# Last feed-forward of a four-layer decoder: its weight work placed beside the cross-attention's units, its output bias added to x by GpSimd

## The chip, the cores and the metric

One core of one Trainium2 chip runs the whole decoder as one program. The metric is the device time of one execution in microseconds; lower is better. Before the change three executions took 3528.01, 3537.2 and 3549.08 us, so the median is 3537.2 us.

## The reference, cut to what matters

The decoder has four layers, each with self-attention, cross-attention and feed-forward, all of the form `x = x + f(layernorm(x))`, on x of 16 x 128 tokens with 256 features in 32-bit floats. The change concerns the end of layer 3. The cross-attention ends with `out @ Wo + bo`. The feed-forward is two linear layers with a GELU between. Each linear layer rounds its weights to 8 bits with one scale for the whole matrix, and adds a low-rank product:

```
def fake_quant_weight(w, bits=8):
    qmax = 2.0 ** (bits - 1) - 1
    scale = jnp.max(jnp.abs(w)) / qmax
    wq = jnp.clip(jnp.round(w / scale), -qmax - 1, qmax) * scale
    return w + stop_gradient(wq - w)

def qat_lora_linear(x, W, b, A, B):        # SCALING = 2
    base = einsum('bsi,oi->bso', x, fake_quant_weight(W)) + b
    lora = einsum('bsr,or->bso', einsum('bsi,ri->bsr', x, A), B)
    return base + SCALING * lora

h = gelu(qat_lora_linear(hidden_states, W_fc, b_fc, A_fc, B_fc))      # 256 -> 1024
h = qat_lora_linear(h, W_proj, b_proj, A_proj, B_proj)                # 1024 -> 256
```

The rank is 16. The kernel folds the low-rank part into the weights: it computes A^T B^T once per weight block and adds twice of it to the rounded block.

## The kernel before, in words

**Tiling.** The 16 sequences are four groups (`NG = 4`) of four (`GB = 4`), 128 tokens each. `self.x[g]` holds the rows of group g, 128 partitions by 4 x 256 features, in SBUF for the whole program. Products are in 32-bit floats; each such matmul of the program appears in the trace as two PE instructions. Small PSUM tiles (`b1`, 128 x 512) rotate through four buffers, so a fifth one waits until the first has been read.

**Order of the instructions.** Each engine works through its own queue in order. A scheduler orders the instructions of a queue from the program; those given to `keep_in_program_order` (through `pinned`, `pinned_transpose` or directly) stay in the order in which they were written. The order that came out of it can be listed per engine, and the prediction uses that of both kernels.

**The last cross-attention** (`xattn64` with 8 heads, called by `l3_xattn`). Sixteen units, one per sequence, are numbered m = 0 to 15. The loop runs m from 0 to 17: iteration m holds on PE the sums of unit m-1 (`sums`, tile d), the scores of unit m (st), the values of unit m-1 (o), the reciprocal row sums spread over the heads (rb), the maxima entered into st, the score products for the next maxima (s), and the projection of unit m-2 (proj). DVE takes the reciprocal r of d (L1200), on which rb waits; multiplies o by rb to cT (L1215), on which the next projection waits; takes the maxima nm of s (L1156), on which st waits in the next iteration; and adds proj to x (L222). ScalarE copies rb (L1213) and takes the exponentials e (L1173). At m = 2, 6 and 10 the next group's prologue follows: keys, the layer norm's transposes (tr), queries and values, with copies by DVE and ScalarE (`evac` alternates between them), bf16 casts kb and qb by GpSimd (L1127, L1135) and the bias `bo` added to x by GpSimd (L1130). `begin` is a function that starts the following feed-forward's work and returns a table "after iteration m do this"; layer 1 uses it (`l1_ffn_begin`: a reduction of each weight, L1281, and roundings, L1294, L1297), layers 2 and 3 do not.

**The last feed-forward** (`l3_ffn`). Loads of the two weights are issued early into slots that the self-attention's last tiles leave free. Everything else starts when the cross-attention's pool closes:

- four loads of the low-rank factors (L2657);
- the largest absolute value of each weight on DVE (L2661), across partitions by a GpSimd `partition_all_reduce` (L2666), scales sc and inv (L2667, L2668);
- three passes of rounding and clipping over each weight, 128 x 2048 (L2671 to L2673);
- 4 low-rank products of 512 columns and 8 of 256 (tile lora), each added to its block by DVE (L2681);
- per group g: layer norm and transposes to hT, 8 blocks of fc with two matmuls each and a GELU to y (L2689), then 4 tiles pr of eight matmuls and one more that adds the bias, from a row of ones and the bias row (L170, in `mm`), `add_x` (L222), and one transfer of x[g] to the output (L2694).

In the order that came out, the layer-norm statistics of groups 0 to 2 and the normalised rows of groups 0 and 1 already stand beside the cross-attention's units; the transposes of all four groups stand after it.

Of the kernel before, what the change touches and what calls it, by code (L numbers as in the profile page):

```python
# [9 lines left out]
F = mybir.dt.float32  # L10
# [3 lines left out]
ALU = mybir.AluOpType  # L14
AX = mybir.AxisListType
PSUM = bass.MemoryType.PSUM

P = 128
B = 16
T = B * P  # L20
DM = 256
DC = 192
NG = 4
GB = B // NG
GT = GB * P
EPS = 1e-5
MAGIC = 12582912.0
# [3 lines left out]
class Decoder:  # L31
# [2611 lines left out]
                finish(*f)  # L2643

    def l3_xattn(self):
        self.xattn64(8, [f"L3_xattn_{n}" for n in ("Wq", "Wk", "Wv", "Wo")], "L3_xattn_bo", "l3x")

    def l3_ffn(self):
        nc = self.nc
        ws = [self.load("L3_W_fcT"), self.load("L3_W_projT")]  # L2650
        bp = self.row("L3_ffn_b_proj")
        outv = self.out.rearrange("(g b s) d -> g s b d", b=GB, s=P)
        with self.tc.tile_pool(name="l3f", bufs=1) as wk:
            lora = {}
            for n, shape in (("A_fc", DM), ("BT_fc", 1024), ("A_proj", 1024), ("BT_proj", DM)):
                lora[n] = wk.tile([16, shape], F, tag=n, name=n)
                nc.sync.dma_start(out=lora[n], in_=self.a[f"L3_{n}"])  # L2657

            mx = wk.tile([P, 2], F, tag="mx", name="mx")
            for i, w in enumerate(ws):  # L2660
                nc.vector.tensor_reduce(  # L2661
                    mx[:, i : i + 1], w.rearrange("p c n -> p (c n)"), AX.X, ALU.max, apply_absolute_value=True
                )
            sc = wk.tile([P, 2], F, tag="sc", name="sc")
            inv = wk.tile([P, 2], F, tag="inv", name="inv")
            nc.gpsimd.partition_all_reduce(sc, mx, P, bass_isa.ReduceOp.max)  # L2666
            nc.vector.tensor_scalar(sc, sc, 1.0 / 127.0, None, ALU.mult)  # L2667
            nc.vector.reciprocal(inv, sc)  # L2668
            for i, (w, a, b) in enumerate(((ws[0], "A_fc", "BT_fc"), (ws[1], "A_proj", "BT_proj"))):
                flat = w.rearrange("p c n -> p (c n)")  # L2670
                nc.vector.tensor_scalar(flat, flat, inv[:, i : i + 1], MAGIC, ALU.mult, ALU.add)  # L2671
                nc.vector.tensor_scalar(flat, flat, -MAGIC, 127.0, ALU.add, ALU.min)
                nc.vector.tensor_scalar(flat, flat, -128.0, sc[:, i : i + 1], ALU.max, ALU.mult)  # L2673
                width = w.shape[2]
                step = min(width, 512)
                for c in range(w.shape[1]):
                    for o in range(0, width, step):
                        ps = self.b1("lora")[:, 0:step]
                        self.mm(ps, [(lora[a][:, c * P : (c + 1) * P], lora[b][:, o : o + step])])
                        wt = w[:, c, o : o + step]  # L2680
                        nc.vector.scalar_tensor_tensor(wt, ps, 2.0, wt, ALU.mult, ALU.add)  # L2681
            wf, wp = ws
            for g in range(NG):
                hT = self.hidden_T(self.layernorm(g))
                y = wk.tile([P, 8, GT], F, tag="y", name="y", bufs=2)
                for c in range(8):
                    ps = self.b1("fc")
                    self.mm(ps, [(wf[:, k, c * P : (c + 1) * P], hT[:, k, :]) for k in range(2)])
                    nc.scalar.activation(y[:, c, :], ps, AF.Gelu, bias=self.c("L3_b_fc")[:, c : c + 1])  # L2689
                for t in range(GB):  # L2690
                    po = self.b1("pr")[:, 0:DM]
                    self.mm(po, [(y[:, c, t * P : (t + 1) * P], wp[:, c, :]) for c in range(8)], bp)
                    self.add_x(g, t, po)
                nc.sync.dma_start(out=outv[g], in_=self.x[g])  # L2694


LAYERS = [
# [121 lines left out]
```

## Time and profile before

| what | value |
|---|---|
| median of the three runs | 3537.2 us |
| the profiled execution | 3545.85 us |
| its span in the trace | 3544.1 us (1.75 us lie around it) |
| its mean granted TensorE clock | 0.975 |
| busy: PE, weight loads, DVE, ScalarE, GpSimd | 3344.9, 1827.0, 2124.5, 1426.0, 426.2 us |
| last cross-attention on PE, to the end of the last proj | 3203 to 3388.2 us |
| between the last proj and the first fc | 3388.2 to 3410.9 us |
| feed-forward products to the end of the span | 3410.9 to 3544.1 us |

Times are microseconds from the start of the span of one profiled execution. PE is TensorE's matmuls, PEld its weight loads, DVE is VectorE, ACT ScalarE, POOL GpSimd, SP the engine that issues most transfers. In a timeline a line has start, duration, engine, line of the kernel, operation, output and inputs, shape, count, and in brackets how long the engine stood idle before it and what released it; "issue" there means that the profile shows nothing that it waited for. The chain of work is followed back from the last instruction, at each step to what released it. The granted clock is the share of TensorE's full clock.

### The profile page before, as it was taken

To read this page: it belongs to the slowest core of one execution; us is meant where nothing else is said; L and a number is where in the kernel's file an instruction comes from. 1 tells how busy PE (TensorE), PEld (TensorE's weight loads), DVE (VectorE), ACT (ScalarE), POOL (GpSimd) and SP (SyncE) were. 2 spreads that over 40 slices of the span, in tenths; PEclk is the share of its full clock that TensorE was granted. 3 is DMA by queue.
4 is the path that set the end of the run, shared out by engine and by line. 5 is a ranking of instruction groups with operands and counts; after the bars stand their busy time and mean duration, and the time that the engine had idled before them with its cause. 6 is when DMAs were issued, how large, how long until landed. Compare 5 with 4: busy or idle time off the path is not lost.

```text
span 3544.1 us, 51931 instructions
## 1 busy us (share of the span) xinstructions
PE 3344.9 (94%) x21208; PEld 1827.0 (52%) x21208; DVE 2124.5 (60%) x4206; ACT 1426.0 (40%) x1908; POOL 426.2 (12%) x571
## 2 busy tenths in 40 slices
PE   7999999999999999998999899978999999999989
PEld 4666655555566566664555566652222222225656
DVE  5546444444565545468677544435999999953430
ACT  2357211111124322238555322124677777783221
POOL 5411000000003211110000110223000000002100
PEclk9979999999999999999999999987999999999989
DMA  2000000000010100010200001655102020000000
GB/s 79 1 23 15 14 23 18 18 23 18 29 50 2 39 1 1 1 43 8 44 1 13 14 1 48 209 186 134 25 12 32 11 32 11 11 1 26 1 8 18
DMA packets 94118, 110.50 MB, mean 31 GB/s; under 512 B 13972, under 2 KB 74006, under 8 KB 93622
## 3 DMA queue, kind: packets, MB, share of 16 engines
q1 hardware_dynamic: 88744, 97.59, 10.4%
q0 software_dynamic: 5136, 9.60, 0.8%
q8 instruction: 167, 2.74, 0.3%
q14 instruction: 71, 0.58, 0.1%
HBM read 91.31 MB, written 15.83 MB: 30 GB/s over the span
## 4 chain that ended last, share of the span: by engine, by line
PE 79%; DVE 10%; ACT 5%; issue 3%; DMA 2%; POOL 1%; SPq 0%; POOLq 0%; ACTq 0%; DVEq 0%
PE acc L2351 7%; PE down L257 7%; PE gate L257 6%; PE up L257 6%; PE proj L257 6%; PE st L2351 5%; PE one L2351 5%; PE st L257 4%; PE qT L168 3%; PE o L257 2%; DVE mx L2497 2%; PE rb L257 2%; PE pr L168 2%; PE kT L1113 2%; PE fc L168 2%
## 5 line engine op out<-in xcount | busy, mean ns | idle before, releaser
L2497 DVE TENSOR_REDUCE mx<-one 128x1 f32<-128x512 f32 x1024 | 658.1, 686 | 55.4 <-PE one L2351 46.0
L2634 ACT ACTIVATE e<-st 128x1024 f32<-128x1024 f32 x512 | 497.1, 1021 | 204.2 <-PE st L2351 203.2
L803 ACT ACTIVATE gs<-gate,cols 128x512 f32<-128x512 f32 x132 | 90.7, 687 | 551.1 <-PE gate L257 544.1
L2351 PE MATMUL acc<-e,v 128*32 128x512 f32 x2048 | 283.7, 608 | 0.9 <-ACT e L2634 0.9
L817 DVE SCALAR_TENSOR_TENSOR x<-down,w_all,x 128x256 f32<-128x256 f32 x512 | 212.3, 477 | 110.4 <-PE down L257 110.2
L2351 PE MATMUL st<-qp,kp 113*128 113x512 bf16 x1024 | 270.6, 384 | 3.6 <-ACT e L2634 1.8
L257 PE MATMUL down<-expert,gs 128*128 128x256 f32 x1056 | 249.4, 379 | 2.2 <-DVE gs L804 2.2
L257 PE MATMUL gate<-hT,expert 128*128 128x512 f32 x528 | 248.5, 593 | 0.2 <-ACT hT L712 0.2
L257 PE MATMUL up<-hT,expert 128*128 128x512 f32 x528 | 248.1, 592 | 0.0
L257 PEld LDWEIGHTS down<-expert,gs 128*128 128x128 f32 x1056 | 200.6, 190 | 85.7 <-issue 61.5
L804 DVE SCALAR_TENSOR_TENSOR gs<-up,cols,gs 128x512 f32<-128x512 f32 x132 | 98.9, 749 | 228.7 <-PE up L257 227.9
L2351 PEld LDWEIGHTS <-qp 16*128 16x128 bf16 x1024 | 48.8, 91 | 329.2 <-issue 317.2
L2351 PE MATMUL one<-kp,qp 16*128 16x512 bf16 x1024 | 210.3, 394 | 6.9 <-DMA kp<-parts 4.2
L257 PEld LDWEIGHTS up<-hT,expert 128*128 128x128 f32 x528 | 100.3, 190 | 126.3 <-issue 126.3
L2351 PEld LDWEIGHTS <-kp 113*128 113x128 bf16 x1024 | 78.7, 98 | 140.3 <-issue 80.1
L1213 ACT COPY rb<-rb 128x512 f32<-128x512 f32 x64 | 37.5, 586 | 264.7 <-PE rb L257 264.7
L257 PEld LDWEIGHTS gate<-hT,expert 128*128 128x128 f32 x528 | 99.6, 190 | 70.3 <-issue 63.5
L1215 DVE TENSOR_TENSOR cT<-o,rb 128x512 f32<-128x512 f32 x64 | 44.2, 691 | 152.5 <-ACT rb L1213 152.5
L168 PE MATMUL qT<-hT,L_xattn_Wq 128*128 128x512 f32 x256 | 114.1, 599 | 4.8 <-DVE hT L112 4.8
L257 PE MATMUL o<-e,v 128*32 128x128 f32 (+1 forms) x2048 | 106.6, 281 | 12.6 <-DVE nm L294 11.8
L1526 DVE SCALAR_TENSOR_TENSOR xs<-xBC,cols,xs 128x508 f32<-128x508 f32 x144 | 105.9, 741 | 14.9 <-ACT xs L1522 11.6
L257 PE MATMUL proj<-L_xattn_Wo,cT 128*128 128x256 f32 x384 | 95.2, 391 | 2.8 <-DVE cT L1215 2.8
(565 smaller groups left out, 5489.4 us busy)
## 6 DMA issues: line engine op xcount, KB each, us to landing
W<-in_L_ffn_W_dram SPq DMA_DIRECT2D x58, 512.0 KB, 4.2
expert<-in_L_ffn_Wg_dram SPq DMA_DIRECT2D x32, 128.0 KB, 2.2
expert<-in_L_ffn_Wu_dram SPq DMA_DIRECT2D x32, 128.0 KB, 2.7
expert<-in_L_ffn_Wd_dram SPq DMA_DIRECT2D x32, 128.0 KB, 2.4
parts<-parts SPq DMA_DIRECT2D x16, 256.0 KB, 2.8
qp<-parts SPq DMA_DIRECT2D x28, 128.0 KB, 3.6
kp<-parts SPq DMA_DIRECT2D x12, 256.0 KB, 7.9
hs<-zero SPq DMA_DIRECT2D x21, 128.0 KB, 4.1
```

Source lines behind the costliest of these rows:

```text
L168: self.nc.tensor.matmul(out, lhsT, rhs, start=i == 0, stop=i == n - 1 and bias is None)
L257: self.tc.keep_in_program_order(self.nc.tensor.matmul(*a, **k))
L803: nc.scalar.activation(gs, pg, AF.Silu, bias=bg)
L804: nc.vector.scalar_tensor_tensor(gs, pu, bu, gs, ALU.add, ALU.mult)
L817: nc.vector.scalar_tensor_tensor(xt, pd[:, t, :], w_all[:, o : o + 1], xt, ALU.mult, ALU.add)
L1113: nc.tensor.matmul(ps, l, r, start=True, stop=False)
L1213: nc.scalar.copy(rb, ps)
L1215: nc.vector.tensor_tensor(cT, po, rb, ALU.mult)
L1526: stt = lambda *a: pin(nc.vector.scalar_tensor_tensor(*a))
L2351: self.tc.keep_in_program_order(nc.tensor.matmul(*a, **k))
L2497: nc.vector.tensor_reduce(mx[:, t, kc, i : i + 1], pair[i], AX.X, ALU.max)
L2634: nc.scalar.activation(e[:, 2 * p : 2 * p + 2, :], ps, AF.Exp, scale=1.0 / 16.0)
```

## The change

The weight work of the last feed-forward becomes `l3_ffn_begin`, handed to the cross-attention as its `begin`. It loads both weights and the low-rank factors (into one slot; those of proj at partition 32) ahead of the cross-attention's bias, and returns the table below. Rows of groups 0 to 2 are normalised and transposed there as well. Those of group 3 follow after the first fc block row (`f["last"]`). The bias matmul of the output is left out; GpSimd adds the bias, loaded to all partitions, to x[g] before the products of the group. The last group's rows go out in four transfers of one sequence each.

```diff
     def l3_xattn(self):
-        self.xattn64(8, [...], "L3_xattn_bo", "l3x")
+        self.xattn64(8, [...], "L3_xattn_bo", "l3x", self.l3_ffn_begin)
+
+    def l3_ffn_begin(self):
+        ws = [self.load("L3_W_fcT"), self.load("L3_W_projT")]
+        lo = self.slot([P, 1280], "lora")
+        for r, parts in ((0, ("A_fc", "BT_fc")), (32, ("A_proj", "BT_proj"))):
+            ...
+                nc.sync.dma_start(out=lo[r : r + 16, c : c + src.shape[1]], in_=src)
+        def largest(i):
+            keep(nc.vector.tensor_reduce(mx[:, i : i + 1], flats[i], AX.X, ALU.max, apply_absolute_value=True))
+        def scales():
+            nc.gpsimd.partition_all_reduce(sc, mx, P, bass_isa.ReduceOp.max)
+            nc.vector.tensor_scalar(sc, sc, 1.0 / 127.0, None, ALU.mult)
+            nc.vector.reciprocal(inv, sc)
+        def rounded(i, step):
+            ...
+        def added(i, cs):
+            ...
+                    self.pinned(ps, lo[r, c * P : (c + 1) * P], lo[r, na + o : na + o + step], start=True, stop=True)
+                    nc.vector.scalar_tensor_tensor(wt, ps, 2.0, wt, ALU.mult, ALU.add)
+        ...
+        def turn(g):
+            hT = self.hp.tile([P, 2, GT], F, tag="hT", name="hT", bufs=5)
+            for k in range(2):
+                ps = self.b1("tr")
+                for t in range(GB):
+                    self.pinned_transpose(ps[:, t * P : (t + 1) * P], hs[g][:, t, k * P : (k + 1) * P])
+                self.evac(hT[:, k, :], ps)
+        st["last"] = lambda: (stats([3]), rows(3), turn(3))
+        return {
+            1: [at(largest, 0)],
+            2: [at(largest, 1), scales],
+            3: [at(rounded, 0, 0)],
+            4: [at(rounded, 0, 1)],
+            5: [at(rounded, 0, 2)],
+            6: [at(rounded, 1, 0)],
+            7: [at(rounded, 1, 1)],
+            8: [at(rounded, 1, 2)],
+            9: [at(added, 0, [0])],
+            10: [at(stats, [0, 1]), at(rows, 0)],
+            11: [at(added, 0, [1])],
+            12: [at(turn, 0)],
+            13: [at(added, 1, [0, 1, 2, 3]), at(rows, 1)],
+            14: [at(stats, [2]), at(rows, 2)],
+            15: [at(turn, 1)],
+            16: [at(added, 1, [4, 5, 6, 7]), at(turn, 2)],
+        }
 
     def l3_ffn(self):
         ...
-            for g in range(NG):
-                hT = self.hidden_T(self.layernorm(g))
+            bp = self.brow(wk, "L3_ffn_b_proj")
+            for g in range(NG):
+                hT = f["hT"][g]
+                nc.gpsimd.tensor_tensor(self.x[g], self.x[g], bp.unsqueeze(1).to_broadcast([P, GB, DM]), ALU.add)
                 ...
+                if g == 0:
+                    f["last"]()
                 for t in range(GB):
                     po = self.b1("pr")[:, 0:DM]
-                    self.mm(po, [(y[:, c, t * P : (t + 1) * P], wp[:, c, :]) for c in range(8)], bp)
+                    self.mm(po, [(y[:, c, t * P : (t + 1) * P], wp[:, c, :]) for c in range(8)])
                     self.add_x(g, t, po)
-                nc.sync.dma_start(out=outv[g], in_=self.x[g])
+                    if g == NG - 1:
+                        nc.sync.dma_start(out=outv[g][:, t, :], in_=self.x[g][:, t, :])
+                if g < NG - 1:
+                    nc.sync.dma_start(out=outv[g], in_=self.x[g])
```

`rounded` does the same three passes as before; `stats` and `rows` do the layer norm as before, with one square root for all groups of a call.

More of the change, by code (lines that the diff above doesn't have):

```diff
@@ L2645, in l3_xattn @@
     def l3_xattn(self):
-        self.xattn64(8, [f"L3_xattn_{n}" for n in ("Wq", "Wk", "Wv", "Wo")], "L3_xattn_bo", "l3x")
-    def l3_ffn(self):
+        self.xattn64(8, [f"L3_xattn_{n}" for n in ("Wq", "Wk", "Wv", "Wo")], "L3_xattn_bo", "l3x", self.l3_ffn_begin)
+    def l3_ffn_begin(self):
         nc = self.nc
         ws = [self.load("L3_W_fcT"), self.load("L3_W_projT")]
[L2651 to L2665, printed above, removed]
+        lo = self.slot([P, 1280], "lora")
+        for r, parts in ((0, ("A_fc", "BT_fc")), (32, ("A_proj", "BT_proj"))):
+            c = 0
+            for n in parts:
+                src = self.a[f"L3_{n}"]
+                nc.sync.dma_start(out=lo[r : r + 16, c : c + src.shape[1]], in_=src)
+                c += src.shape[1]
+        vals = self.wp.tile([P, 12], F, tag="l1f", name="l3w")
+        mx, sc, inv = vals[:, 0:2], vals[:, 2:4], vals[:, 4:6]
+        flats = [w.rearrange("p c n -> p (c n)") for w in ws]
+        st = {"ws": ws, "hT": {}}
+        self.l3f = st
+        keep = self.tc.keep_in_program_order
+        def largest(i):
+            keep(nc.vector.tensor_reduce(mx[:, i : i + 1], flats[i], AX.X, ALU.max, apply_absolute_value=True))
+        def scales():
             nc.gpsimd.partition_all_reduce(sc, mx, P, bass_isa.ReduceOp.max)
@@ L2668, in l3_ffn @@
             nc.vector.reciprocal(inv, sc)
[L2669 to L2681, printed above, removed]
@@ L2682, in l3_ffn @@
-            wf, wp = ws
+        def rounded(i, step):
+            w = flats[i]
+            if step == 0:
+                keep(nc.vector.tensor_scalar(w, w, inv[:, i : i + 1], MAGIC, ALU.mult, ALU.add))
+            elif step == 1:
+                keep(nc.vector.tensor_scalar(w, w, -MAGIC, 127.0, ALU.add, ALU.min))
+            else:
+                keep(nc.vector.tensor_scalar(w, w, -128.0, sc[:, i : i + 1], ALU.max, ALU.mult))
+        def added(i, cs):
+            r = slice(32 * i, 32 * i + 16)
+            na = (DM, 1024)[i]
+            width = ws[i].shape[2]
+            step = min(width, 512)
+            for c in cs:
+                for o in range(0, width, step):
+                    ps = self.b1("lora")[:, 0:step]
+                    self.pinned(ps, lo[r, c * P : (c + 1) * P], lo[r, na + o : na + o + step], start=True, stop=True)
+                    wt = ws[i][:, c, o : o + step]
+                    nc.vector.scalar_tensor_tensor(wt, ps, 2.0, wt, ALU.mult, ALU.add)
@@ new lines, in l3_ffn_begin, with stats @@
+        hs = {}
+        def stats(gs):
+            n = len(gs)
+            mv = self.small([P, n, GB, 2], "l1mv")
+            rs = self.small([P, n, GB], "l1rs")
+            for i, g in enumerate(gs):
+                bs = self.small([P, GB, 6], "bnst")
+                for t in range(GB):
+                    nc.vector.bn_stats(bs[:, t, :], self.x[g][:, t, :])
+                    nc.vector.bn_aggr(mv[:, i, t, :], bs[:, t, :])
+            self.rsqrt(rs, mv[:, :, :, 1])
+            for i, g in enumerate(gs):
+                hs[g] = mv[:, i], rs[:, i]
@@ new lines, in rows @@
+        def rows(g):
+            mv, rs = hs[g]
+            h = self.hp.tile([P, GB, DM], F, tag="h", name="h", bufs=2)
+            for t in range(GB):
+                nc.vector.tensor_scalar(
+                    h[:, t, :], self.x[g][:, t, :], mv[:, t, 0:1], rs[:, t : t + 1], ALU.subtract, ALU.mult
+                )
+            hs[g] = h
+        def turn(g):
+            hT = self.hp.tile([P, 2, GT], F, tag="hT", name="hT", bufs=5)
+            for k in range(2):
+                ps = self.b1("tr")
+                for t in range(GB):
+                    self.pinned_transpose(ps[:, t * P : (t + 1) * P], hs[g][:, t, k * P : (k + 1) * P])
+                self.evac(hT[:, k, :], ps)
+            st["hT"][g] = hT
@@ new lines, in l3_ffn_begin @@
+        st["last"] = lambda: (stats([3]), rows(3), turn(3))
+        at = lambda f, *a: lambda: f(*a)
+        return {
[16 more added lines that the diff above has]
+        }
@@ L2683, in l3_ffn @@
+    def l3_ffn(self):
+        nc = self.nc
+        f = self.l3f
+        wf, wp = f["ws"]
+        outv = self.out.rearrange("(g b s) d -> g s b d", b=GB, s=P)
+        with self.tc.tile_pool(name="l3f", bufs=1) as wk:
+            bp = self.brow(wk, "L3_ffn_b_proj")
             for g in range(NG):
-                hT = self.hidden_T(self.layernorm(g))
+                hT = f["hT"][g]
+                nc.gpsimd.tensor_tensor(self.x[g], self.x[g], bp.unsqueeze(1).to_broadcast([P, GB, DM]), ALU.add)
```

## Prediction, made before the changed kernel ran

> **What bounds the kernel now.** I read first the busy times by stage, then the chain of work that ended last, then the timeline of the last 340 us, and last, for prices, the timeline of the first layer's cross-attention, which already carries weight work beside its units.
>
> The busy times in three stretches (columns: length; PE, weight loads, DVE, ACT, POOL busy with instructions; granted TensorE clock; DMA):
>
> ```profile
> core 0: us, PE busy (x) PEld busy (x) DVE busy (x) ACT busy (x) POOL busy (x), PEclk, DMA share, GB/s
> 3203.00:3388.20 185.20, 178.85 (x1496) 114.80 (x1494) 84.45 (x149) 53.79 (x73) 29.95 (x42) 1.00 0.02 7
> 3388.20:3410.90 22.70, 14.95 (x32) 8.68 (x32) 19.12 (x27) 0.30 (x1) 0.37 (x1) 0.59 0.03 7
> 3410.90:3544.10 133.20, 127.58 (x441) 79.25 (x440) 11.48 (x27) 25.51 (x37) 0.00 (x0) 0.99 0.05 16
> ```
>
> The reader is to see three regimes. In the last cross-attention PE is busy 97% and DVE 46%. Then come 22.7 us of DVE work on the feed-forward weights. Then 133 us of feed-forward, bound by PE again. The chain shows what the middle and the end consist of:
>
> ```profile
> 3386.20 2.01 PE proj L257 x8
> 3388.57 4.48 DVE mx L2661 x2
> 3394.11 1.29 DVE L_W_fcT L2671
> ...
> 3401.91 7.19 PE lora L168 x16
> 3409.10 1.90 PE tr L185 x8
> 3410.99 14.80 PE fc L168 x32
> 3425.80 3.45 PE pr L168 x16
> 3429.25 0.62 PE pr L170 x2
> 3429.87 3.65 PE pr L168 x16
> 3434.15 3.65 PE pr L168 x16
> ```
>
> From the end of the last proj to the first fc nothing of the products runs. And each output tile costs 3.65 + 0.62 = 4.27 us, of which the bias row (L170) is a part.
>
> **What goes.** (1) The stretch 3388.19 to 3410.93, 22.7 us: in the changed order PE's first fc follows the last proj directly, with the rows of groups 0 to 2 turned and the weights finished. (2) The bias matmuls. Without them a tile is 16 instructions at 0.214 us (half of the 0.4285 us at which the 128x512 fc instructions follow each other), 3.43 us against 4.275. That is 0.845 x 16 = 13.5 us. The bounds are 0.43 us a tile (the row's two instructions alone) and 0.85 (with the two pauses of 0.33 us in the weight loads around them); I take the upper one, since fc to pr, both 128 rows high, shows no such pause. (3) Between groups, turning and copying hT stops PE from 3442.69 to 3444.07 and once more for 0.1 us: 1.5 x 3 = 4.5 us, less one group's transposes, which stay inside the tail (0.9). (4) The first fc group is 0.9 us slow at the lowered clock. Items 2 to 4 are 18.0, which checks another way: 3410.93 to the last PE instruction's end at 3539.52 is 128.6; the changed tail is 4 x 13.71 (fc) + 4 x 13.71 (pr) + 0.9 = 110.6. (5) The last output transfer is a quarter (128 KB); the issue table has 2.2 us for 128 KB and 2.9 for 512: 0.7 us. Gain: 22.7 + 18.0 + 0.7 = 41.4 us.
>
> **What it costs beside the units.** There PE is the bound, so every added PE instruction is on the path, and DVE work counts only where the reciprocal r comes late, because rb waits for it in PE's order with everything behind it. The first layer shows exactly this:
>
> ```profile
> 1354.18 0.64 PE L257 MATMUL d<-e,pick 128*32 128x128 f32 x16
> 1354.62 2.28 DVE L1281 TENSOR_REDUCE p<-L_ffn_w_up 128x16 f32<-128x2048 f32 x1
> 1356.82 0.95 DVE L1200 RECIPROCAL r<-d 128x128 f32<-128x128 f32 x1
> 1357.82 1.16 PE L257 MATMUL rb<-r,spread 128*128 128x128 f32 x8 [0.88 <-DVE l1f L1285]
> 1361.61 0.64 PE L257 MATMUL d<-e,pick 128*32 128x128 f32 x16
> ```
>
> A unit with the 2.28 us reduction lasts 7.43 us; plain ones last 6.48.
>
> Maxima. Unit 1 has no projection ahead of r: r would start at 3232.4 instead of 3230.1, rb at 3233.4 instead of 3232.0: 1.4 us. The second stands behind a prologue, where the first layer's like case (reduction at 1347.20, rb at 1350.39 with 1.14 of idle) gives 1.2.
>
> Roundings, six of 1.22 to 1.29 us (L2671 to L2673). In the row above one microsecond less makes r ready in time, so five cost nothing (cover: st and o, 2.1 us; uncovered they would cost 1.25 each). The one behind a prologue costs 0.2.
>
> Low-rank sums. 8 instructions of 512 columns and 16 of 256: 3.43 + 3.43 us. Their own row is dearer, 7.19 for the sixteen. The Trainium skill ("TensorE: Matmul & The Clock Gate", Part 1, "What's actually happening") says an idle window of about 3.4 us halves the array's clock and as long a busy one restores it. The trace grants 0.50 from 3393 to 3410.9 and 1.00 throughout 3203 to 3388.2. By their own rows (5.96 + 7.19) the sums would cost 13.2, at the units' clock 6.9; I take the latter plus 0.4 per group for the change of height, as the bias row shows it. Three groups lie inside units: 3 x 2.1 = 6.3. DVE's additions (0.68 and 0.42 each) run while PE is on the sums. The fourth group lies before the last proj, where PE now idles 1.4 us for cT. There the third sum reuses o's PSUM buffer and so waits for cT; with 8 transposes behind it proj slips from 3386.2 to about 3388.7: 2.5.
>
> Transposes. Two further groups inside units, 1.0 each: 2.0. The row statistics and rows were already beside the units in before, with three table-load pairs instead of now two; I count nothing either way (cover: proj and st; at most 2.6 us).
>
> GpSimd. Its queue puts the four bias adds of the new kernel after all casts. The skill ("GPSIMD Engine Reference", 4.1) speaks against this: a two-input add belongs on VectorE, GpSimd being about twice as slow. The trace has 2.36 us for the same add (L1130). By the rule some 1.2 us a group are thrown away; but add x of group 0 is due only 17 us after its bias lands (13.7 of fc, 3.4 of pr), so both prices are zero here. Uncovered it is 2.4. The order of the first prologue's GpSimd work changes, two qb casts now stand ahead of the xattn bias adds; from the casts' 0.6 and the adds' 2.36 the last qb ends at 3220.5 instead of 3218.5, when s wants it at 3220.1: 0.4.
>
> The all-reduce of the maxima needs another GpSimd library; the order shows its unnamed loading instruction after the second prologue's casts, and another after the last casts. The only price in the trace is the start, where GpSimd stands still for 9.99 us:
>
> ```profile
> 11.14 0.28 POOL masks.py:199 TENSOR_SCALAR_AFFINE_SELECT ident<-ident 128x128 f32<-128x128 f32 x1 [9.99 <-issue]
> ...
> 3250.81 0.61 POOL L1135 CAST qb<-qT 128x512 bf16<-128x512 f32 x1 [0.99 <-ACT qT L114]
> ```
>
> Loaded from 3251.4, it is there at 3261.4, and the reduction adds 0.4. sc on DVE waits for that; behind it are cT, the next nm, add x, the first rounding and the next r, and PE waits for r. Counting these (5.7 us in all) back from the next rb at 3266.2, loading is free up to 9.1 us: 0.9 at 10. Bounds: 0 and the whole 10. The second loading has 45 us.
>
> SP issues four small loads (0.4 us each) ahead of the xattn bias; from 3201.6 they end at 3203.2, before that bias is due at 3203.5: nothing, at most 1.6.
>
> Cost: 1.4 + 1.2 + 0.2 + 6.3 + 2.5 + 2.0 + 0.4 + 0.9 = 14.9 us. Net 41.4 - 14.9 = 26.5.
>
> **Rivals.**
> A, the sum above: span 3544.1 - 26.5 = 3517.6, the profiled execution 3545.85 - 26.5 = 3519.4. The three runs shown have their median 8.65 us below that execution, so I subtract from the median: 3537.2 - 26.5 = 3510.7. Chance 0.66 (3502 to 3519).
> B, the inserted steps do stop PE: five roundings at the 0.95 of the larger row, low-rank sums near their own rows (6 more): 10.8 more cost, 3521.5. For it: every step is queued before r. Against it: the slack computed above, and the clock. Chance 0.18.
> C, the products do not start where the order has them, because y's room is freed late or Gelu's table (1.28) and the last group's root stand before it: fc would halt after four PSUM buffers. By my times Gelu is ready 3 us after the last proj and the fifth fc needs it after 6.9. If 8 us were lost, 3518.7. Chance 0.11.
> D, slower: the library. Its loading stands before sc, sc before all of DVE, and each microsecond beyond 9.1 is a microsecond of PE. From 36 us on (26.5 + 0.9 + 9.1) the kernel is slower; at 50 us it would be 3551. The start row speaks against it: it needs only 10. Chance 0.05.
> That the change does not do what it says has little room: the order shows the sums and turns beside the units and no bias matmul.
>
> **How the numbers follow.** Forecast 3510.7. 0.5% (17.7 us) is about what a measurement of this kernel can tell from no change; the limit is 3519.5. A lies below it nearly wholly (0.63 of 0.66), B to a quarter (0.05), C to more than half (0.07), and a gain beyond A's bound is in A: faster 0.75. The rest but D and a hundredth of unforeseen loss is no change: 0.19; slower 0.06. The range 3498 to 3524 takes B and C in and, below, waits that turn out covered (the 2.6, 2.5 and 0.9 above) with the scatter of the runs shown (10 us either way).
>
> **What would show it.** Right: no stretch of PE under half busy after 3200, clock 1.00 to the end; first fc within 0.3 us of the last proj; add x every 3.43 us; that first fc at about 3403; rb waiting about 1.2 to 1.4 us twice; the tail, first fc to last pr, 110.6. Wrong: an idle PE ahead of rb in units with roundings (B), ahead of the fifth fc or Gelu (C), or DVE waiting for sc (D); or low-rank matmuls of 0.86 us.

## The result, and the profile after

The changed kernel takes 3506.89 us, the median of seven runs (3491.51 to 3511.1). Seven runs of the kernel before have the median 3537.2 us (3526.98 to 3549.08). The ratio is 0.9906, with a 95% interval of 0.9878 to 0.9934: faster by 0.94%, against a forecast of 3510.7 us.

The profiled execution took 3510.04 us (span 3508.3). That is 35.8 us below the profiled execution of before, but not all of it belongs to the change. The last product of layer 3's self-attention (tile acc) ends at 3201.26 us before and at 3195.56 after, and nothing ahead of it was edited: 5.7 us of the difference arose there. From that point on I compare lengths of stages. Three runs with the changed kernel's cross-attention (the run after and two experiments below) agree to 0.02 us in the stages that they share. The end of the span is read to 0.1 us, so lengths up to it are good to 0.05 us.

| stage, us | before | after | change | predicted |
|---|---|---|---|---|
| last acc to end of last proj | 186.93 | 198.48 | +11.55 | +14.9 |
| to the first fc | 22.74 | -0.16 | -22.90 | -22.7 |
| first fc to end of last pr | 128.59 | 111.22 | -17.37 | -18.0 |
| to the end of the span | 4.58 | 3.20 | -1.38 | -0.7 |
| sum | 342.84 | 312.74 | -30.10 | -26.5 |

The busy times by stage of the changed kernel, with the columns that the table of before had (length; PE, weight loads, DVE, ACT, POOL busy; granted clock; DMA). The first stretch starts at the transfer of the cross-attention's bias, 2.28 us behind the last acc:

```profile
3197.84:3394.00 196.16, 188.79 (x1543) 121.47 (x1542) 104.54 (x177) 52.33 (x73) 29.81 (x42) 1.00 0.03 7
3394.00:3505.10 111.10, 111.10 (x393) 73.48 (x391) 9.60 (x24) 24.35 (x36) 9.30 (x4) 1.00 0.06 19
3505.10:3508.30 3.20, 0.00 (x1) 0.00 (x0) 0.42 (x1) 0.00 (x0) 0.00 (x0) 1.00 0.12 41
```

The middle regime of before, 22.7 us at a clock of 0.59, has gone. In the feed-forward PE is busy 111.10 of 111.10 us at full clock. The same is seen in the timeline at the border of the two stages (start, duration, engine, line, operation):

```profile
3388.24 1.13 PE L257 MATMUL rb<-r,spread 128*128 128x128 f32 x8 [0.33 <-DVE l1mv L2706]
3389.30 1.99 PE L257 MATMUL lora<-lora 16*128 16x256 f32 x8
...
3391.22 1.09 PE L260 MATMUL tr<-ident,h 128*128 128x128 f32 x8
...
3392.15 1.89 PE L257 MATMUL proj<-L_xattn_Wo,cT 128*128 128x256 f32 x8
...
3393.88 6.60 PE L168 MATMUL fc<-hT,L_W_fcT 128*128 128x512 f32 x15
...
3397.17 4.67 POOL L2759 TENSOR_TENSOR x<-x,L_ffn_b_proj 128x1024 f32<-128x1024 f32 x2 [54.96 <-DVE h L2715]
```

Sums, a turn (the transposes of one group), the last proj and the first fc follow one another without a bracket, that is, without idle time ahead of them. GpSimd's first bias adds run beside the first fc block. The chain of work, whose end before held DVE's weight work, bias rows (L170) and transposes, now holds nothing but products and the last group's transposes from the first fc on, up to the last add. It begins:

```profile
3394.04 13.73 PE fc L168 x32
3407.77 0.87 PE tr L260 x8
3408.65 13.81 PE pr L168 x64
3422.46 13.73 PE fc L168 x32
```

Two units lost time as foreseen, where a maximum stands ahead of r. This is the first; the second waits 1.14 us:

```profile
3224.41 2.28 DVE L2668 TENSOR_REDUCE l3w<-L_W_fcT 128x1 f32<-128x2048 f32 x1
...
3226.61 0.95 DVE L1200 RECIPROCAL r<-d 128x128 f32<-128x128 f32 x1
...
3227.61 1.16 PE L257 MATMUL rb<-r,spread 128*128 128x128 f32 x8 [1.23 <-DVE r L1200]
```

### The profile page after: what moved, and what is told of

It is laid out like the page before. It is cut to its first block, busy times and chain, and to the rows that moved or that the text cites. A ratio compares the mean times of both kernels' runs of the same rounds, so it can differ in the third digit from the quotient of the medians.

```text
span 3508.3 us, 51877 instructions
## 1 busy us (share of the span) xinstructions
PE 3319.3 (95%) x21176; PEld 1813.7 (52%) x21176; DVE 2122.5 (61%) x4205; ACT 1423.0 (41%) x1905; POOL 436.2 (12%) x575
## 4 chain that ended last, share of the span: by engine, by line
PE 80%; DVE 11%; ACT 4%; issue 2%; DMA 1%; POOL 1%; SPq 0%; ACTq 0%; POOLq 0%; DVEq 0%
PE acc L2351 7%; PE down L257 7%; PE gate L257 6%; PE up L257 6%; PE proj L257 6%; PE st L2351 5%; PE one L2351 5%; PE st L257 4%; PE qT L168 4%; PE o L257 2%; DVE mx L2497 2%; PE rb L257 2%; PE v L1113 2%; PE kT L1113 2%; PE pr L168 2%
## 5 line engine op out<-in xcount | busy, mean ns | idle before, releaser
L257 PE MATMUL o<-e,v 128*32 128x128 f32 (+1 forms) x2048 | 105.8, 279 | 12.6 <-DVE nm L294 11.8
```

Source lines behind the costliest of these rows:

```text
L257: self.tc.keep_in_program_order(self.nc.tensor.matmul(*a, **k))
```

## Experiments

Ratios are to runs of the kernel before taken beside each experiment, with medians of 3537 to 3539 us. My theory was the sum of the prediction with its terms as measured. The rivals were that the inserted work stops PE more than counted (B), that products start late (C, which the profile after refutes already: no idle PE in the feed-forward), and that the GpSimd library is the danger (D). Each experiment takes one term by itself. All stages are given as in the table above: acc to proj, gap, tail, end, sum.

| kernel | acc to proj | gap | tail | end | sum | median, us (ratio to before, interval) |
|---|---|---|---|---|---|---|
| before | 186.93 | 22.74 | 128.59 | 4.58 | 342.84 | |
| after | 198.48 | -0.16 | 111.22 | 3.20 | 312.74 | 3506.89 (0.9906, 0.9878 to 0.9934) |
| bias only | 186.94 | 31.67 | 116.83 | 4.61 | 340.05 | 3531.57 (0.9977, 0.9963 to 0.9990) |
| bias only, behind the all-reduce | 188.46 | 22.74 | 115.57 | 4.62 | 331.39 | 3519.59 (0.9946, 0.9930 to 0.9963) |
| weights only | 195.85 | 1.22 | 127.80 | 4.64 | 329.51 | 3523.94 (0.9959, 0.9943 to 0.9975) |
| rows back in the tail | 195.83 | 1.23 | 114.91 | 3.22 | 315.19 | 3499.18 (0.9897, 0.9863 to 0.9930) |
| sums back behind proj | 191.96 | 9.41 | 113.24 | 3.24 | 317.85 | 3504.84 (0.9900, 0.9864 to 0.9936) |
| the same, 128 rows high | 192.00 | 6.73 | 111.23 | 3.15 | 313.11 | 3502.78, one run |
| one last transfer | 198.49 | -0.17 | 111.23 | 4.62 | 314.17 | 3491.33, one run |
| library ahead of the all-reduce | 198.49 | -0.16 | 111.22 | 3.20 | 312.75 | 3496.06, one run |
| maxima behind r | 195.97 | -0.16 | 111.23 | 3.13 | 310.17 | 3494.21 (0.9892, 0.9869 to 0.9916) |
| maxima behind r, sums 128 rows high | 195.18 | -0.16 | 111.22 | 3.15 | 309.39 | 3496.27 (0.9886, 0.9862 to 0.9909) |

The medians scatter by some 10 us either way for a reason that lies ahead of the change (last section), so the verdicts below rest on the stages.

**1. The bias alone, by GpSimd.** On the kernel before:

```diff
+            bp = self.brow(wk, "L3_ffn_b_proj")
             ...
+                nc.gpsimd.tensor_tensor(self.x[g], self.x[g], bp.unsqueeze(1).to_broadcast([P, GB, DM]), ALU.add)
-                    self.mm(po, [(y[:, c, ...], wp[:, c, :]) for c in range(8)], bp)
+                    self.mm(po, [(y[:, c, ...], wp[:, c, :]) for c in range(8)])
```

> The kernel before with one part of the change alone: the output bias is added to x by GpSimd and the bias matmuls are gone; the weight work, the layer norm and the one last store stand as before. My theory (a bias matmul costs its own two instructions and the two pauses of the weight loads around it, 0.82 to 0.85 us a tile): the stretch from the first fc to the last pr falls from 128.6 to about 115.3 us (16 x 0.83 = 13.3), add x follows add x by 3.45 us. Rival (only the two instructions themselves, 0.43 us a tile, the pauses staying somewhere else): 121.7 us. Second rival (GpSimd's adds come late or hold VectorE up): less than 13 gained and add x waiting for GpSimd by name. The gap between last proj and first fc stays at 22.7, and total against the kernel before: -13 or -7.

The tail fell by 11.8 us, nearer my 13.3 than the rival's 6.9; most of the rest is the clock, which stays at 0.50 for the first 3.9 us of this tail and for the first 1.8 us of that of before (by an estimate from these two, 1.0 us). But the gap, which every theory had at 22.7, grew to 31.67, and the sum fell by only 2.8 us. GpSimd's timeline of this run names the cause:

```profile
3387.93 4.64 POOL L2685 TENSOR_TENSOR x<-x,L_ffn_b_proj 128x1024 f32<-128x1024 f32 x2 [48.66 <-DMA L_ffn_b_proj<-in_L_ffn_b_proj_dram]
3398.23 0.37 POOL L2666 PARTITION_ALL_REDUCE sc<-mx  x1 [5.67 <-issue]
```

The scheduler put two bias adds ahead of the all-reduce. They wait for the bias's transfer, take 4.64 us, and push the loading of the all-reduce's library (5.67 us, shown as "issue") behind them. The trace has a MODIFY_POOL_CONFIG, an instruction of the all-reduce's line, at the start of this idle time, at 3392.5; in the kernel before it stands at 3343.5, 50 us ahead of the all-reduce. All of DVE's roundings wait for that all-reduce.

**2. The same with the adds behind the all-reduce** (`keep` holds the written order).

```diff
-            nc.gpsimd.partition_all_reduce(sc, mx, P, bass_isa.ReduceOp.max)
+            keep(nc.gpsimd.partition_all_reduce(sc, mx, P, bass_isa.ReduceOp.max))
             ...
-                nc.gpsimd.tensor_tensor(self.x[g], ...)
+                keep(nc.gpsimd.tensor_tensor(self.x[g], ...))
```

> The kernel before with the bias alone by GpSimd, as in the run with the bias only, but the four bias adds held behind the all-reduce of the maxima in GpSimd's queue. In that run two adds (4.64 us) and a library loading (5.67) stood ahead of the all-reduce, and the gap between last proj and first fc was 31.67 us in place of 22.74. If this queue is the cause, the gap is back at 22.7 (+-0.2), the tail stays at 116.8, and from the end of the last acc to the end of the span it is 331 us against 342.8 in the kernel before. If it is something else (the wait for the bias's transfer, VectorE), the gap stays above 28.

The gap is back at 22.74, the tail is 115.57, the sum 331.39: the queue was the cause. The two kernels' gaps differ by 8.93 us through the order of one queue. The bias matmuls are worth 13.02 us of tail here (128.59 to 115.57), 0.81 a tile, or 12.8 us without the half clock at the start of both tails (1.8 us of it before, 1.3 here).

Acc to proj came out 1.5 us longer, in a stretch without an edit. That is the clock: the eight products of the last proj took 3.52 us in place of 1.99. In all twelve traces the granted clock changes on a grid of 3.41 us, which lies differently in each run, and here a step of that grid with much idle time ended just behind the start of the last proj:

```profile
3385.13:3388.55 3.42, 1.79 (x15) 1.34 (x12) 1.23 (x3) 1.65 (x2) 0.00 (x0) 1.00 0.00 0
3388.55:3391.96 3.41, 3.22 (x8) 2.02 (x6) 0.15 (x1) 0.22 (x1) 0.00 (x0) 0.50 0.00 0
3391.96:3395.37 3.41, 0.00 (x0) 0.00 (x0) 3.41 (x3) 0.00 (x0) 0.00 (x0) 1.00 0.34 87
```

After a step with 1.79 us of PE the clock is 0.50, after one with 3.22 it is 1.00. Where the limit lies is not shown: the run of experiment 1 has a step with 1.79 us of PE (from 3378.77) and stays at 1.00 behind it.

GpSimd's queue in this run:

```profile
3396.88 0.38 POOL L2667 PARTITION_ALL_REDUCE sc<-mx  x1 [51.55 <-DVE mx L2661]
3404.32 5.03 POOL L2686 TENSOR_TENSOR x<-x,L_ffn_b_proj 128x1024 f32<-128x1024 f32 x2 [7.07 <-issue]
```

The library now changes back behind the all-reduce (7.07 us), where no one waits for it.

**3. The weights' work alone.** The changed kernel with `rows`, `turn` and `stats` taken out of the table, the bias matmul and the single transfer restored:

```diff
-            10: [at(stats, [0, 1]), at(rows, 0)],
             ...
-            12: [at(turn, 0)],
             ...
-                hT = f["hT"][g]
+                hT = self.hidden_T(self.layernorm(g))
-                    ... for c in range(8)])
+                    ... for c in range(8)], bp)
```

> The changed kernel with only the weights' work beside the units: maxima, roundings and low-rank sums as in the changed kernel; layer norms and turns of all four groups, bias matmuls and the single last transfer as in the kernel before. My theory: the gap between last proj and first fc falls from 22.7 to about 2.5 us (the first group's turn, 8 transposes and two copies); the tail from the first fc is 128.6 less 0.9 us of low clock, about 127.7; the units cost 1.27 + 1.2 + 0.2 + 3 x 1.91 = 8.4 us and the fourth group of sums ahead of the last proj about 0.5 (proj waits 1.4 us for its operand there anyway). Together about 12 us faster than before (20.2 + 0.9 - 8.9). Rival (roundings and sums do stop PE elsewhere and the change's gain comes mainly from the tail): the units cost over 14 us and the gain is under 7.

Acc to proj grew by 8.92 us (expected 8.9), the tail is 127.80 (127.7), and the gap 1.22 instead of 2.5: behind the transposes the first fc waits only for the first copy of hT, and the second copy is done beside it.

```profile
3392.66 2.84 PE L168 MATMUL fc<-hT,L_W_fcT 128*128 128x512 f32 x6 [0.35 <-DVE hT L112]
```

The sum is 13.33 us below before, so over two fifths of the gain is this part alone. Rival B, over 14 us of cost, falls.

**4. The rows and turns back in the tail,** each group ahead of its products; the rest as in the changed kernel (the table without `stats`, `rows` and `turn`, `hidden_T(self.layernorm(g))` as above, and `f["last"]` left out).

> The changed kernel with the layer norms' rows and turns of all four groups back in the tail, each ahead of its group, as before the change. My theory: between the units 2 x 0.9 us of turns disappear and 0.9 ahead of the last proj; in the tail the first group's turn opens a gap of about 2.5 us between last proj and first fc, and the three later groups cost 1.5 us each in place of the last group's 0.9. Tail first fc to last pr about 114.8 (111.2 - 0.9 + 4.5), total about +3.4 us against the changed kernel. Rival (turning beside the units is free of price there and the tail's pauses are covered by PSUM buffers that are ready): between 0 and +1 us.

Acc to proj fell by 2.65 us, the gap rose by 1.39 and the tail by 3.69: the sum is 2.45 us above the changed kernel (3.4 expected; the gap is what came out smaller). Turning beside the units pays, but little, since what leaves the tail is largely paid for beside the units. Against experiment 3 this kernel has the bias by GpSimd and four last transfers: tail 12.89 lower, end 1.42 lower.

**5. All low-rank sums behind the last proj.**

```diff
-            9: [at(added, 0, [0])],
             ...
-            11: [at(added, 0, [1])],
             ...
-            13: [at(added, 1, [0, 1, 2, 3]), at(rows, 1)],
+            13: [at(rows, 1)],
             ...
-            16: [at(added, 1, [4, 5, 6, 7]), at(turn, 2)],
+            16: [at(turn, 2)],
+            17: [at(added, 0, [0, 1]), at(added, 1, list(range(8)))],
```

> The changed kernel with all 24 low-rank instructions taken out of the units and put between the last proj and the first fc, maxima and roundings staying beside the units. Clock theory: PE has had no idle stretch there, the granted clock stays at 1.00, so the sums last about 7 us (8 x 0.43 + 16 x 0.21) and the first fc comes about 7.5 to 8 us behind the last proj; the units lose 3 x 1.91 and the last proj 0.4, net +1 to +2 us against the changed kernel, and the sums' rows show 0.43 and 0.21 us an instruction. Rival (the rows of the kernel before, 0.75 and 0.45 us an instruction, are what such sums cost where they stand in a row, for instance because VectorE's additions free the PSUM buffers too slowly): the sums last 13 us and the net is about +7.

Neither theory holds. The sums took 9.4 us, the net is +5.1 us. Stretches of this run (same columns as before):

```profile
3374.00:3384.50 10.50, 9.16 (x78) 7.39 (x76) 4.81 (x11) 3.40 (x5) 0.00 (x0) 1.00 0.00 0
3384.50:3387.70 3.20, 3.20 (x13) 1.72 (x12) 2.70 (x6) 0.30 (x1) 0.00 (x0) 0.98 0.20 41
3387.70:3393.92 6.22, 6.14 (x16) 3.65 (x13) 4.54 (x11) 0.00 (x0) 5.99 (x3) 0.50 0.01 3
3393.92:3397.40 3.48, 3.48 (x5) 1.51 (x5) 1.72 (x4) 0.00 (x0) 2.60 (x2) 0.50 0.00 0
3397.40:3507.16 109.76, 109.76 (x389) 72.98 (x387) 7.01 (x16) 23.75 (x34) 0.78 (x1) 1.00 0.06 18
```

Cut at the places where the clock changes:

```profile
3384.15:3387.57 3.42, 3.42 (x14) 1.78 (x12) 2.57 (x6) 0.30 (x1) 0.00 (x0) 1.00 0.19 38
3387.57:3397.81 10.24, 10.16 (x21) 5.47 (x18) 6.40 (x15) 0.00 (x0) 9.00 (x4) 0.50 0.01 2
```

The first sums run at full clock. After 3.1 us of them, with PE busy all the time, the granted clock halves, and it comes back 3.9 us into the full-height fc products. My clock theory had said that only an idle PE loses its clock.

**6. The same sums, 128 rows high.** The factors stand in one zeroed tile, and each product runs over all 128 partitions; the rows without a factor are zero in one of the two operands.

```diff
-        lo = self.slot([P, 1280], "lora")
+        lo = self.slot([P, 1536], "lora")
+        nc.vector.memset(lo, 0.0)
         ...
-                    self.pinned(ps, lo[r, c * P : ...], lo[r, na + o : ...], start=True, stop=True)
+                    self.pinned(ps, lo[:, a + c * P : ...], lo[:, na + o : ...], start=True, stop=True)
```

> The run with all low-rank sums between last proj and first fc, but each of the 24 products over all 128 rows, the rows that hold no factor being zero in one operand (a zeroing of the 128x1536 tile by VectorE at the start of the cross-attention is added; the values are the same). With 16 rows the granted clock fell to 0.50 after 3.3 us of them, though PE was busy throughout; the stretch from last proj to first fc was 9.41 us. If the height of the products is what the clock follows: clock 1.00 all through, 24 products in 6.9 us, first fc 7.2 us behind the last proj, tail 111.2 instead of 113.24. If the clock fell because of the pauses of PE before (proj waiting 1.0 us) or of PE waiting for VectorE's additions: as with 16 rows, 9.4 and 113.2.

The height decides. The same 24 products now take 7.05 us, the gap is 6.73, the tail 111.23:

```profile
3379.80:3386.50 6.70, 6.70 (x24) 4.40 (x24) 6.29 (x14) 0.30 (x1) 3.57 (x2) 1.00 0.07 20
```

That the grid of the clock lies elsewhere in this run is not the reason: two whole steps of it (3379.71 to 3386.54) are filled with these sums and the clock stays, where one step of low ones was enough in experiment 5. The step ahead is alike in both, with PE busy for 2.40 of 3.41 us. With full height, sums behind proj cost only 0.4 us more in all than sums beside the units (313.11 against 312.74). At 16 rows the same choice of place was worth 5.1. The kernel before had its sums in the dear form: 7.19 us of them passed at a clock of 0.50 throughout.

**7. One last transfer** in place of four:

```diff
-                    if g == NG - 1:
-                        nc.sync.dma_start(out=outv[g][:, t, :], in_=self.x[g][:, t, :])
-                if g < NG - 1:
-                    nc.sync.dma_start(out=outv[g], in_=self.x[g])
+                nc.sync.dma_start(out=outv[g], in_=self.x[g])
```

> The changed kernel with one transfer of 512 KB for the last group, as before the change, in place of four of 128 KB. My first sum (medians of the issue table, 2.9 us for 512 KB and 2.2 for 128 KB): the stretch from the end of the last pr to the end of the span grows by 0.7 us from 3.2. Rival (what the two profiles show, 4.56 before and 3.2 after, is the transfer's doing and not scatter): it grows by 1.36 to about 4.56.

The end is 4.62 us, 1.42 more: the rival was right. In the table, too, every kernel with one last transfer ends in 4.6 us and every one with four in 3.1 to 3.2. The last issue of before stands at 3540.01, 4.1 us ahead of its span's end; that of after at 3505.59, 2.7 ahead. The 2.9 us of the issue table fit: a transfer of 512 KB to the output landed 2.9 us after its issue. But the 2.2 us belong to another kind of transfer, the 32 loads of `expert` into SBUF, and other rows of 128 KB in the same table have 2.4 to 4.1. The kernel before had no output transfer of 128 KB to read a time from.

**8. The library put directly ahead of the all-reduce.**

```diff
+            nc.gpsimd.tensor_tensor(mx, mx, mx, ALU.add)
             nc.gpsimd.partition_all_reduce(sc, mx, P, bass_isa.ReduceOp.max)
-            nc.vector.tensor_scalar(sc, sc, 1.0 / 127.0, None, ALU.mult)
+            nc.vector.tensor_scalar(sc, sc, 1.0 / 254.0, None, ALU.mult)
```

> The changed kernel with one tiny GpSimd addition (128x2 on itself; the factor of the scale is halved for it, so the values are the same) directly ahead of the all-reduce of the maxima. The addition needs VectorE's second maximum, and the library for the all-reduce can only be loaded behind it, where the changed kernel loads it 7.5 us earlier, behind the casts. If a library costs what the start of the kernel shows (9.99 us): the scale comes some 10 to 11 us later than in the changed kernel, VectorE's queue and with it the reciprocal and PE stand still, and PE loses about 5 to 9 us in that unit. Rival (a loaded library is nearly free in mid-kernel, the 9.99 us of the start being something else): the scale comes 1 us later and PE loses 0 to 0.5 us.

```profile
3240.46 0.19 POOL L2671 TENSOR_TENSOR l3w<-l3w 128x2 f32<-128x2 f32 x1 [7.45 <-DVE l3w L2668]
...
3245.99 0.94 DVE L1200 RECIPROCAL r<-d 128x128 f32<-128x128 f32 x1
3246.29 0.37 POOL L2672 PARTITION_ALL_REDUCE l3w<-l3w  x1 [5.64 <-issue]
```

The loading takes 5.64 us in mid-kernel, not the 9.99 of the start. PE lost nothing, but this says less than the expectations meant: the scheduler also moved the scale on DVE behind the next r, so nothing that PE needs stood behind it. What a late scale ahead of cT would have cost was not tried. The size is enough for rival D: 5.64 us is below the 9.1 that the prediction had found free, and in the changed kernel the all-reduce started 7.50 us after GpSimd's cast, released by DVE's maximum.

**9. The maxima behind r.** A hook `beside.get((m, "r"))` directly after `r = sums(es[m - 1])`, and in the table:

```diff
-            1: [at(largest, 0)],
-            2: [at(largest, 1), scales],
-            3: [at(rounded, 0, 0)],
+            (2, "r"): [at(largest, 0)],
+            (3, "r"): [at(largest, 1)],
+            3: [scales],
+            4: [at(rounded, 0, 0)],
```

The later roundings follow one unit later.

> The changed kernel with the two maxima (2.28 us each) moved behind the reciprocal r in VectorE's queue, in units that have no maximum ahead of r; scales and roundings one unit later. My theory (PE loses time only because r stands behind the long reduction in VectorE's queue): the two idle times of 1.23 and 1.14 us ahead of rb go, and the stretch from the last cross-attention's bias to the last proj is 2.0 to 2.4 us shorter. Rival (VectorE's total occupancy in that unit is what is late, so the reduction delays cT, st and the next nm instead): the stretch is unchanged within 0.4 us and an idle time appears at o or proj.

```profile
3204.89 0.95 DVE L1200 RECIPROCAL r<-d 128x128 f32<-128x128 f32 x1
3205.75 2.23 DVE L2670 TENSOR_REDUCE l3w<-L_W_fcT 128x1 f32<-128x2048 f32 x1
...
3206.78 1.16 PE L257 MATMUL rb<-r,spread 128*128 128x128 f32 x8
```

The reduction is as long as before, and rb no longer waits (no bracket). Acc to proj is 2.51 us shorter. The price of the maxima was their place in the queue, nothing else.

**10. The best version: 9 with the sums beside the units 128 rows high** (the diff of 6).

> The changed kernel with the two maxima behind r (as in the run before) and the low-rank products beside the units 128 rows high. If a change of height costs about 0.2 us per group, the three groups inside units last 1.72 in place of 1.91 and the stretch from last acc to last proj falls from 195.97 to about 195.4; the zeroing (some 1 to 1.6 us of VectorE, in the stretch where the weights are loaded) costs 0 to 1 us. Rival: the 0.2 us are the weight loads' own and stay, and the zeroing makes it a loss: 196 to 197.

Acc to proj fell to 195.18, 0.79 below experiment 9. Eight products last 1.88 us instead of 1.98, and as much again goes at the change of height: a unit with sums lasts 8.19 us instead of 8.39. The zeroing (1.34 us on DVE) cost nothing that can be seen. From the last acc this kernel is 3.3 us shorter than the changed one and 33.4 shorter than before. The medians (3496.27 against 3506.89) do not tell these two kernels apart, since the intervals of their ratios overlap.

## Why the prediction was right, and where its terms were off

**The gap** (22.7 us): right. First fc stands directly behind the last proj.

**The bias rows** (13.5): measured 13.02 (experiment 2) and 12.89 (3 against 4), 0.81 us a tile. The choice of the upper bound was right; the lower bound of 6.9 is refuted. The bound's own working does not close: two instructions (0.43) and two pauses of 0.33 would be 1.09 us, not 0.85. The 0.85 is the measured tile less sixteen products, and it is this figure that held. The rest of the tail, 4.5 less 0.9 for the turns and 0.9 for the clock, came out as 3.69 and 0.79. The three measured parts, 12.89 + 3.69 + 0.79, make the whole 17.37; the tail of 110.6 became 111.2, since a tile takes 3.455 us and not 3.43.

**The last transfer** (0.7) was mis-sized: 1.4. The step that failed took a median of loads into SBUF, 2.2 us, for an output transfer of the same size (experiment 7).

**The costs** (14.9) were too high by 3.4 us:

| term | predicted | measured |
|---|---|---|
| two maxima | 2.6 | 2.5 |
| rounding behind a prologue; the other five | 0.2; 0 | 0.2; 0 |
| three groups of sums | 6.3 | 5.7 |
| sums and turn ahead of the last proj | 2.5 | 1.35 |
| two turns | 2.0 | 1.8 |
| order of qb casts | 0.4 | 0 |
| library | 0.9 | 0 |

The waits ahead of rb that the prediction named as its sign, 1.2 to 1.4 us twice, were 1.23 and 1.14. Five units with roundings followed each other at 6.47 to 6.48 us, as plain ones do. In the sums the change of height cost 0.2 us a group and not the 0.4 taken from the bias row. "There the third sum reuses o's PSUM buffer and so waits for cT" failed: the eight products ahead of the last proj took 1.99 us, as long as elsewhere. The library was sized by the only price in the trace of before, the 9.99 us of the start; it takes 5.64. The last qb did end where the prediction had it, 16.84 us behind the issue of the bias transfer (3220.5 meant 16.97), but what it held up cost nothing: the score products stretched from 0.39 to 0.61 us, and nm, which is what the next step waits for, started at its old distance of 17.33 us.

Net: 26.5 predicted, 30.1 measured; 3.4 of the difference are costs, 0.7 the transfer, 0.2 the gap, -0.6 the tail. The median predicted from it, 3510.7, would have been 3507.1 with the measured terms; it was 3506.89. So close an agreement is luck, as the seven runs spread over 20 us; what the prediction had right is seen in the stages. The first fc, forecast at about 3403, came at 3393.88: 5.7 us from the stretch ahead of the change and 3.4 from the smaller costs.

**The clock.** The prediction rested on the Trainium skill ("TensorE: Matmul & The Clock Gate", Part 1, "What's actually happening"): an idle window of about 3.4 us halves the clock. For the kernel as changed that gave nearly the right price: the clock was 1.00 throughout, which fits groups of sums only 2 us long between full products. As a rule for sums elsewhere it was incomplete: 3.1 us of products 16 rows high did the same as idleness (experiment 5), and full height undid it (6). The measurement decides. The trace of before agrees: 7.19 us of busy PE in its second row of sums did not bring the clock back from 0.50. The skill's other rule, that a two-input add belongs on VectorE ("GPSIMD Engine Reference", 4.1), was not put to the test: DVE is busy for 9.60 of the 111.10 us of feed-forward, so the adds might have been hidden there too, and no run tried it. What the runs show is that four adds of 9.30 us on GpSimd lay wholly beside PE and replaced 13 us on PE. Their place in GpSimd's queue mattered (experiment 1); in the changed kernel that danger does not arise, since the all-reduce stands over 140 us ahead of the adds.

## What to carry to other kernels

Work for a second engine that stands between two stages of the bounding one is best put beside the earlier stage, but each piece by its place in the queue: behind the instruction for which the bounding engine waits, not ahead of it. A part of a change can be worth 2.8 us or 11.5 alone, depending on what it displaces in a queue that the bounding engine does not even use; list that queue's order before pricing the part. Low matmuls in a row were dear twice here, by their clock (experiment 5) and by the change of height (experiment 10), and padding them with zeros to full height, where the rows stand empty, cost nothing that could be seen.

## What the hardware showed that was not expected

Products of 16 rows in a row did to the granted clock what idleness does: 1.00 to 3387.57, then 0.50 for 10.24 us, with PE busy in 10.16 of them, the last 3.9 already on full-height products (experiment 5). At 128 rows the same products kept 1.00 (experiment 6; one profile of each).

A GpSimd library costs 5.64, 5.67 and 7.07 us in three places, and 9.99 at the start.

The scatter of the runs goes with the clock. By the clock records of the traces the clock stood at 0.50 for 154 us ahead of 3160 us in the profiled execution of before, for 147 in that of after, and for between 113 and 171 in the experiments. The last acc ended at 3175.4 us with 113 and at 3203.3 with 171. Most of it lies at 180 to 240 us and at 2400 to 2500. PE is not idle there: in the run after it is busy for 26.20 of the 27.00 us from 188 and for 68.64 of the 76.00 from 2416, at a clock of 0.50 and 0.51. Among its products there are 75 that are 16 rows high, which would fit experiment 5, but no run tests it. The Trainium skill ("TensorE: Matmul & The Clock Gate", Part 1, "What's actually happening") calls the window free-running, so that the point of change moves from run to run. The traces agree: the changes of clock lie 3.41 us apart or a multiple of it, and at other places in each run. That this is what makes the length of the half clock differ is not tested.

It stays open why the medians of five experiments (rows in the tail, sums behind proj, bias behind the all-reduce, both with maxima behind r) lie 8 to 12 us further below the median of before taken beside them than their stages account for. The surplus lies ahead of the changed stages, in unchanged code, and has the size of this scatter.
